# Cross-attention in 160 slots: the order of the low parts, the bias addition and the fill's last value pass

## The chip, the cores and the metric

One core of a Trainium2 chip. The metric is the device time of one execution in microseconds (us); of several runs the median counts. The engines are named as in the profile: PE (TensorE, matmuls) with PEld (its weight loads), DVE (VectorE), ACT (ScalarE), POOL (GpSimd) and SP (SyncE, which issues nearly all DMAs here).

## The reference

The inputs are x (32 batches of 512 rows of 640) and a context (32 batches of 77 rows of 1024). The context has exactly 77 rows, so the three further key segments of the reference are empty, and what is left is one attention with 20 heads of 32, an output projection, a bias and a residual:

```python
q = _heads(hidden_states @ to_q_w)
s = jnp.einsum('bhqd,bhkd->bhqk', q, k) * scale
p = jax.nn.softmax(s, axis=-1)
h = jnp.einsum('bhqk,bhkd->bhqd', p, v)
out = _merge(h) @ to_out_w + to_out_b
out = (out + residual) / RESCALE        # RESCALE = 1.0
```

Everything is float32. The kernel multiplies in the type fp32r and gets its precision back by splitting each operand into a high part (a cast to fp32r) and a low part (the operand minus its high part), and by adding three products: high with high, high with low, low with high.

## The kernel before, in words

**Ahead of the main loop** (up to about 265 us of the span) the keys and values of all batches are computed in four groups of columns, split, and written to scratch in DRAM (k_dram, v_dram). The main part then works in 160 slots, `slot(n)`, n = 5 b + j: b is the batch of 512 query rows and j one of five chunks of four heads.

**One slot** works on several stages at once, for different n:

- scores of slot n, four groups of 128 query rows, t = 0 to 3: three matmuls each (L464), then VectorE's negated row maximum (L472); `exps` runs four exponentials per group on ScalarE (L482), which also sum.
- queries of slot n+1: 15 matmuls (L445) in two portions of 6 and 9; `split_q` makes high (ScalarE, L102) and low (VectorE, L103).
- probabilities of slot n-1: `sums` takes the reciprocals on VectorE (L492), `normalize` multiplies on POOL (L497), `transpose_p` transposes 32x32 blocks on VectorE (L504) and writes them to DRAM with four DMAs (pd, L511).
- slot n-2's transposed probabilities are loaded again, `load_p`: three DMAs (L521, L523) into `raw`, three planes of 512.
- slot n-3 is "taken" (LAG = 3): `cast_p` makes the high parts of all three planes on ScalarE (L529); `rest_p` the low parts of planes 0 and 1 on VectorE (L535); `last_p` copies two quarters with POOL (L542, L543) and makes the low part of plane 2 there (lp, L545); `values` runs four matmuls into the bank pa (L554), reading planes 0, 1, 3 and 4 of pp in turn; `sum_a` adds four head quarters (ScalarE copy L578, two additions on VectorE, L580).
- slot n-4's last value pass: one more matmul with lp (`rest_values`, L566), after which `high_a` (ScalarE, L587) and `low_a` (VectorE, L592) leave the attention output `at`; `low_a` also frees pa, which has one buffer.
- output projection of an earlier batch: 24 matmuls per slot (L610) in two pieces after a fixed table (STEPS, CUTS, PIECES), into two PSUM banks `po`. `finish` adds a closed bank to the residual tile xr on VectorE (L639) and stores finished rows (L645). That residual is loaded one slot earlier (`load_residual`, L599), and POOL adds the bias to it (`add_bias`, L603), in the slots with j = 2, 3, 4 and 0.
- x of the next batch: loads (L251), transposes on VectorE (L255), `split_x` with high parts on ScalarE (L262) and low parts on POOL (L263), in the slots with j = 2 (two chunks) and j = 3 (three).
- keys and values of the next group are loaded into kb and vb by SP, `refill` in two halves (L417 in j = 1 and 2, L425 in j = 0 and 3); `copy_values` copies within vb on POOL in j = 1 and 4 (L433, L435).

[...] In the main loop the order ahead of scores group 1 is

```python
s = scores(n, 0)
if n:
    normalize(n - 1, sums(n - 1))
if taken is not None:
    rest_p(taken)
if taken is not None:
    last_p(taken)
```

with `cast_p` before it and `add_bias` far behind it, after the second half of `refill`, `finish` and `load_residual`.

**The fill** is the slots in which a value pass is taken but no projection is there yet: n = 3 to 6 (`filling`). Slot 7 (NC_ + 2) is the first with a projection. After the last slot `end()` works off what is left, with the same helpers.

## Time and profile before

| what | value |
| --- | --- |
| runs, median (lowest to highest) | 2008.37 us (2007.27 to 2008.49), 3 runs |
| the profiled execution, its own time | 2004.05 us |
| its span | 2002.3 us |
| instructions in it | 36798 |
| granted TensorE clock, mean | 0.993 |
| DMA | 448.34 MB, mean 224 GB/s |

The span runs from the first to the last instruction of the profiled execution; its own time is a little longer than the span, and lies just below the three timed runs. In the tables of the profile a row names line, engine, operation and tiles (out<-in) and gives times in us or ns; "idle before" is idle time of that engine just ahead of such instructions, with what ended it, and a releaser is inferred from the semaphores, so with several waits it is the one that came last.

### The profile page before, as it was taken

How to read it: one execution, taken by the hardware profiler on the slowest of the kernel's cores; microseconds unless marked ns; L12 is line 12 of the kernel's file. 1: busy time of each engine (PE TensorE's matmuls, PEld its weight loads, DVE VectorE, ACT ScalarE, POOL GpSimd, SP SyncE). 2: the span in 40 equal slices, each digit the busy share in tenths (PEclk: the TensorE clock that was granted, in tenths of full speed). 3: DMA queues.
4: the chain of work that ended last, by engine and by line, in shares of the span. 5: the costliest groups of instructions: out<-in, count | busy, mean ns of one | idle time of the engine just before them, and what ended most of it. 6: DMA issues, size and time to landing. Idle time of an engine off the chain costs nothing.

```text
span 2002.3 us, 36798 instructions
## 1 busy us (share of the span) xinstructions
PE 1896.2 (95%) x10172; PEld 1668.2 (83%) x10172; DVE 1596.7 (80%) x2334; ACT 1525.0 (76%) x6050; POOL 1448.0 (72%) x1308
## 2 busy tenths in 40 slices
PE   9999996999999999999999999999999999999997
PEld 7888985888888888888888888888888888888886
DVE  4444447888888888889888888888888888888885
ACT  3232247888888888888888888888888888888883
POOL 1000156788788888888888888888888888888875
PEclk9999997999999999999999999999999999999999
DMA  9888788888888888888888888888888888888975
GB/s 189 210 187 244 178 226 205 219 232 218 228 234 234 225 230 229 232 229 242 222 241 229 237 231 223 236 237 228 224 238 236 232 223 231 230 230 230 240 212 156
DMA packets 561436, 448.34 MB, mean 224 GB/s; under 512 B 177296, under 2 KB 459344, under 8 KB 561232
## 3 DMA queue, kind: packets, MB, share of 16 engines
q1 hardware_dynamic: 556720, 431.50, 83.0%
q0 software_dynamic: 4416, 14.34, 2.1%
q8 instruction: 82, 1.34, 0.3%
q14 instruction: 122, 1.00, 0.2%
q10 hardware_dynamic: 96, 0.16, 0.0%
HBM read 264.21 MB, written 181.64 MB: 223 GB/s over the span
## 4 chain that ended last, share of the span: by engine, by line
PE 30%; DMA 21%; ACT 20%; issue 12%; DVE 10%; SPq 5%; POOL 2%; DVEq 0%; ACTq 0%; POOLq 0%
PE pq L445 9%; ACT pn L482 8%; DMA raw<-pd 8%; DMA xs<-in_x_dram 8%; PE po L610 7%; ACT pp L529 6%; PE pv L190 4%; PE sc L464 4%; PE pk L190 4%; SPq L511 3%; ACT aw L578 3%; DMA pd<-z 3%; DVE z L504 3%; DVE nm L472 3%; ACT xt L262 2%
## 5 line engine op out<-in xcount | busy, mean ns | idle before, releaser
L482 ACT ACTIVATE pn<-sc,nm 128x77 f32<-128x77 f32 x2560 | 802.2, 335 | 205.2 <-DVE nm L472 201.2
L610 PE MATMUL po<-wo_s,at 128*128 128x320 f32 x3840 | 640.5, 312 | 54.3 <-DVE at L592 28.4
L610 PEld LDWEIGHTS po<-wo_s,at 128*128 128x128 f32 x3840 | 576.0, 188 | 79.8 <-DVE xr L639 41.8
L445 PE MATMUL pq<-xt,wq_s 128*128 128x512 f32 x2400 | 611.1, 396 | 0.0
L497 POOL TENSOR_TENSOR pn<-pn,rs 128x1232 f32<-128x1232 f32 x160 | 387.7, 2423 | 242.2 <-DVE rs L492 155.8
L482 ACT ACTIVATION_READ_ACCUMULATOR pn<-sc,nm 128x1 f32 x2560 | 545.9, 213 | 0.0
L445 PEld LDWEIGHTS pq<-xt,wq_s 128*128 128x128 f32 x2400 | 440.1, 190 | 76.9
L535 DVE TENSOR_TENSOR pp<-raw,pp 96x1024 fp32r<-96x1024 f32 x160 | 355.8, 2224 | 140.2 <-ACT pp L529 134.0
L464 PE MATMUL sc<-kb,qt 128*128 128x308 f32 x1920 | 380.6, 307 | 28.1 <-DMA kb<-k_dram 16.3
L464 PEld LDWEIGHTS sc<-kb,qt 128*128 128x128 f32 x1920 | 325.3, 189 | 77.2 <-ACT pn L482 13.9
L472 DVE TENSOR_REDUCE nm<-sc 128x4 f32<-128x308 f32 x640 | 294.0, 460 | 30.6 <-PE sc L464 27.5
L529 ACT CAST pp<-raw 128x1536 fp32r<-128x1536 f32 x160 | 237.5, 1484 | 30.2 <-DMA raw<-pd 27.7
L580 DVE TENSOR_TENSOR pa<-pa,aw 64x512 f32<-64x512 f32 x320 | 222.5, 695 | 47.2 <-ACT aw L578 38.9
L504 DVE STREAM_TRANSPOSE z<-pn 128x1280 f32<-128x1280 f32 x160 | 239.0, 1494 | 2.1 <-POOL pn L497 1.9
L263 POOL TENSOR_TENSOR xt<-xs,xt 128x512 fp32r<-128x512 f32 x160 | 202.7, 1292 | 35.8 <-ACT xt L262 35.5
L542 POOL CAST pp<-pp 32x512 fp32r<-32x512 f32 x160 | 211.0, 1319 | 18.9 <-ACT pp L529 8.4
L545 POOL TENSOR_TENSOR lp<-raw,pp 128x512 fp32r<-128x512 f32 x160 | 207.0, 1294 | 12.9
L603 POOL TENSOR_TENSOR xr<-xr,bias 128x640 f32<-128x640 f32 x128 | 200.7, 1569 | 2.5
L554 PE MATMUL pa<-pp,vb 128*128 128x512 f32 x640 | 176.9, 397 | 3.9 <-DVE at L592 2.1
L578 ACT COPY aw<-pa 64x1024 f32<-64x1024 f32 x160 | 161.8, 1011 | 20.3 <-PE pa L554 16.5
L211 POOL DMA_DIRECT2D k_dram<-ks x20 | 14.5, 727 | 190.0 <-DVE ks L103 190.0
L190 PE MATMUL pk<-ct,wk_s 128*128 128x512 f32 (+1 forms) x600 | 134.2, 382 | 1.7 <-ACT wk_s L102 0.9
(48 smaller groups left out, 1783.1 us busy)
## 6 DMA issues: line engine op xcount, KB each, us to landing
pd<-z SPq DMA_DIRECT2D x640, 160.0 KB, 3.5
raw<-pd SPq DMA_DIRECT2D x160, 512.0 KB, 4.2
xs<-in_x_dram SPq DMA_DIRECT2D x128, 320.0 KB, 6.0
raw<-pd SPq DMA_DIRECT2D x320, 128.0 KB, 4.2
xr<-in_x_dram SPq DMA_DIRECT2D x128, 320.0 KB, 4.2
out_dram<-xr SPq DMA_DIRECT2D x127, 320.0 KB, 3.8
v_dram<-vs SPq DMA_DIRECT2D x80, 192.0 KB, 4.1
k_dram<-ks POOLq DMA_DIRECT2D x20, 512.0 KB, 4.1
```

The source lines that it names most:

```text
L190: nc.tensor.matmul(held[j][:, :gn], w[:, k, a, :], cts[g, k][:, c, :gn], start=(k == 0 and n == 0), stop=(k == NK - 1 and n == 2),)
L445: nc.tensor.matmul(pqs[n], wq_s[:, k, a, j * P : (j + 1) * P], xts[b, k][:, c, :], start=(k == 0 and m == 0), stop=(k == NC_ - 1 and m == 2),)
L464: nc.tensor.matmul(sc[:, :KCOLS], qt[:, a, t * P : (t + 1) * P], kb[:, j - GROUPS[g][0], c], start=(m == 0), stop=(m == 2),)
L472: nc.vector.tensor_reduce(nm, sc[:, :KCOLS].rearrange("p (h k) -> p h k", k=NKEY), AX.X, ALU.max, negate=True)
L482: nc.scalar.activation(pnb[n % 2][:, at, :NKEY], sc[:, i * NKEY : (i + 1) * NKEY], AF.Exp, bias=nm[:, i : i + 1], accum_out=sms[n][:, at : ...
L497: nc.gpsimd.tensor_tensor(pf, pf, rs.unsqueeze(2).to_broadcast([P, NQ * HPC, NKEY]), ALU.mult)
L504: nc.vector.transpose(z.rearrange("p b t j -> p t b j"), pn.rearrange("p (t h) k -> p t (h k)", t=NQ).rearrange("p t (b i) -> p t b i", i=Q),)
L529: nc.scalar.copy(pp[:, 0:3, :], raws[n])
L535: nc.vector.tensor_tensor(pp[:96, 3:5, :], raw[:96, 0:2, :], pp[:96, 0:2, :].bitcast(F32), ALU.subtract)
L578: nc.scalar.copy(aw, pa[64:])
L580: nc.vector.tensor_tensor(pa[64 * p : 64 * p + 64, 0], pa[:64, p], aw[:, p], ALU.add)
L610: nc.tensor.matmul(pos[b, t, h][:, :HALF], ats[b * NC_ + j][:, a, t * P : (t + 1) * P], wos[0][:, j, c, h * HALF : (h + 1) * HALF], start= ...
```

## The change

It changes the order in the slot, and one cast:

- `cast_p`: the cast of three planes becomes two instructions, planes 0 and 1 first, then plane 2.
- `slot`: `rest_p` (L535, VectorE) moves ahead of the reciprocals of `sums` (L492) and so ahead of `normalize` in program order; the two are on VectorE and POOL.
- `add_bias` moves from after `load_residual` to right after scores group 0, ahead of `rest_p`, `normalize` and `last_p`; on POOL it is now ahead of L497. The tile it adds to is the same, loaded in the slot before.
- fill: the last value pass and `high_a`, `low_a` (`taken_parts`) come after the second portion of the queries instead of around scores group 1, in slots with `filling` and in slot 7 (`FIRST_OUT`); in the fill slot with j = 1 both halves of `refill` (four DMAs of keys) come right after the first portion of the queries, ahead of `load_p`.

```diff
     def cast_p(n):
 
         pp = late[0].tile([P, 5, S], FPR, tag="pp", name="pp", bufs=1)
-        nc.scalar.copy(pp[:, 0:3, :], raws[n])
+        nc.scalar.copy(pp[:, 0:2, :], raws[n][:, 0:2, :])
+        nc.scalar.copy(pp[:, 2, :], raws[n][:, 2, :])
         pps[n] = pp
...
     LATE = 2
+    FIRST_OUT = NC_ + 2
     LAG = 3
...
         s = scores(n, 0)
+        if j in BIAS and b >= BIAS[j][0]:
+            add_bias(b - BIAS[j][0], BIAS[j][1])
+        if taken is not None:
+            rest_p(taken)
         if n:
             normalize(n - 1, sums(n - 1))
-        if taken is not None:
-            rest_p(taken)
         if taken is not None:
             last_p(taken)
...
         if ahead:
             queries(n + 1, 0, 2)
-        if n - 1 in takes:
+        if filling and j == 1:
+            refill(b, j, 0)
+            refill(b, j, 1)
+        late_rest = filling or n == FIRST_OUT
+        if n - 1 in takes and not late_rest:
             rest_values(takes[n - 1])
         s = scores(n, 1)
-        if n - 1 in takes:
+        if n - 1 in takes and not late_rest:
             taken_parts(takes[n - 1], rest=False)
         if n - LAG + 1 in pds and n > LATE:
             load_p(n - LAG + 1)
-        if filling:
+        if filling and j != 1:
             refill(b, j, 0)
...
-        refill(b, j, 1)
+        if not (filling and j == 1):
+            refill(b, j, 1)
         finish()
...
-        if j in BIAS and b >= BIAS[j][0]:
-            add_bias(b - BIAS[j][0], BIAS[j][1])
         exps(n, 1, *s)
...
             queries(n + 1, 2, NC_)
+        if n - 1 in takes and late_rest:
+            taken_parts(takes[n - 1])
         s = scores(n, 2)
```

## The prediction

> **What bounds the kernel now.** I read the page's busy shares first, then the busy time by stretch for the steady part, then TensorE's timeline over one batch, and last the other engines' timelines over the same batch. First the row of the busy shares, then the row of the steady stretch (us, then busy time and instructions of PE, PEld, DVE, ACT and POOL, granted clock, DMA share, GB/s).

> ```profile
> PE 1896.2 (95%) x10172; PEld 1668.2 (83%) x10172; DVE 1596.7 (80%) x2334; ACT 1525.0 (76%) x6050; POOL 1448.0 (72%) x1308
> ```

> ```profile
> 376.00:1909.00 1533.00, 1462.69 (x8120) 1298.94 (x8119) 1337.01 (x1943) 1313.25 (x5366) 1273.59 (x1131) 1.00 0.87 231
> ```

> A steady batch issues 5 x 56 = 280 matmuls, so 8120 of them are 29 batches: 1533/29 = 52.86 us each. TensorE is the busiest engine, at full clock, but no slot kind is full by itself; where it still waits is seen in one batch. I call a slot by its j, kind 0 to 4, and give times from its first scores matmul (L464). Columns: start, duration, engine, line; in brackets the idle time.

> ```profile
> 1381.54 0.59 PE L464 MATMUL sc<-kb,qt 128*128 128x308 f32 x3
> ...
> 1388.28 1.09 PE L554 MATMUL pa<-pp,vb 128*128 128x512 f32 x4
> 1389.21 0.59 PE L464 MATMUL sc<-kb,qt 128*128 128x308 f32 x3
> ...
> 1391.30 1.14 PE L610 MATMUL po<-wo_s,at 128*128 128x320 f32 x6 [0.64 <-DVE xr L639]
> 1392.28 0.59 PE L464 MATMUL sc<-kb,qt 128*128 128x308 f32 x3
> ...
> 1397.27 2.29 PE L610 MATMUL po<-wo_s,at 128*128 128x320 f32 x12
> ...
> 1402.51 0.59 PE L464 MATMUL sc<-kb,qt 128*128 128x308 f32 x3
> ...
> 1405.04 0.47 PE L566 MATMUL pa<-lp,vb 128*128 128x512 f32 x1 [0.55 <-ACT pp L529]
> ...
> 1410.06 1.10 PE L554 MATMUL pa<-pp,vb 128*128 128x512 f32 x4
> ...
> 1413.17 0.58 PE L464 MATMUL sc<-kb,qt 128*128 128x308 f32 x3
> ...
> 1419.74 0.86 PE L610 MATMUL po<-wo_s,at 128*128 128x320 f32 x4 [1.13 <-DVE at L592]
> 1420.44 1.09 PE L554 MATMUL pa<-pp,vb 128*128 128x512 f32 x4
> ...
> 1424.43 0.59 PE L464 MATMUL sc<-kb,qt 128*128 128x308 f32 x3
> ...
> 1434.28 0.59 PE L464 MATMUL sc<-kb,qt 128*128 128x308 f32 x3
> ```

> The differences of the L464 rows are the slots: 10.74, 10.23, 10.66, 11.26 and 9.85 us. Every slot has the same 56 matmuls, and kind 4 runs without a gap, so 9.85 is TensorE's own time and 52.86 - 5 x 9.85 = **3.6 us of waiting per batch**. Here it is 0.89 in kind 0 (a projection bank that L639 empties), 0.38 in kind 1 (the same, inside the 2.29), 0.81 in kind 2 (L566 adds into the bank that the sums L580 write; the row names a cast beside it), 1.41 in kind 3 (the low part L592). All four end with an instruction of VectorE (in other batches kind 1 also waits for keys, in kind 2's stead). Why VectorE is late there:

> ```profile
> 1383.43 0.23 DVE L492 RECIPROCAL rs<-sm 128x16 f32<-128x16 f32 x1
> 1384.40 2.70 DVE L535 TENSOR_TENSOR pp<-raw,pp 96x1024 fp32r<-96x1024 f32 x1 [0.74 <-ACT pp L529]
> ...
> 1390.78 0.47 DVE L639 TENSOR_TENSOR xr<-po,xr 128x320 f32<-128x320 f32 x1
> ...
> 1405.34 1.15 DVE L535 TENSOR_TENSOR pp<-raw,pp 96x1024 fp32r<-96x1024 f32 x1
> ...
> 1415.54 3.16 DVE L535 TENSOR_TENSOR pp<-raw,pp 96x1024 fp32r<-96x1024 f32 x1 [1.10 <-ACT pp L529]
> ```

> ```profile
> 1381.75 1.57 POOL L603 TENSOR_TENSOR xr<-xr,bias 128x640 f32<-128x640 f32 x1
> 1383.74 2.28 POOL L497 TENSOR_TENSOR pn<-pn,rs 128x1232 f32<-128x1232 f32 x1 [0.42 <-DVE rs L492]
> 1386.09 1.49 POOL L542 CAST pp<-pp 32x512 fp32r<-32x512 f32 x1
> 1387.63 0.61 POOL L543 CAST pp<-pp 32x512 fp32r<-32x512 f32 x1
> ...
> 1405.56 3.07 POOL L497 TENSOR_TENSOR pn<-pn,rs 128x1232 f32<-128x1232 f32 x1 [3.94 <-PE pa L566]
> ...
> 1412.85 2.54 POOL L263 TENSOR_TENSOR xt<-xs,xt 128x512 fp32r<-128x512 f32 x2
> ...
> 1422.76 3.79 POOL L263 TENSOR_TENSOR xt<-xs,xt 128x512 fp32r<-128x512 f32 x3
> ```

> The low parts L535 take 1.15 us when they start before the normalization L497 (1405.34, 0.22 ahead of it), and L497 then takes 3.07 instead of 2.28. When L497 is already running, L535 ends 1.08 after it whatever it started with: 1384.40 + 2.70 = 1387.10 against 1383.74 + 2.28 = 1386.02. So the two exclude each other, and the copy L542 pays too (1.49 against 0.61 for L543 of the same shape). In kind 0 L535 ends at 5.56 and VectorE then runs back to back to L639 (end 1391.25); in kind 3 it ends at 5.53 and L592 follows. **The present order makes VectorE pay for the normalization.**

> [...]

> **The change, part by part.** *Low parts ahead of the reciprocals, the cast in two parts.* The chain to the next values is now serial: values of the slot before, sums copy L578, four exponentials, first part of the cast, L535, L492, L497, L542, L543, values. Its remaining durations:

> ```profile
> 1411.25 1.01 ACT L578 COPY aw<-pa 64x1024 f32<-64x1024 f32 x1
> 1412.16 0.62 ACT L262 CAST xt<-xs 128x512 fp32r<-128x512 f32 x1
> ...
> 1414.02 1.49 ACT L529 CAST pp<-raw 128x1536 fp32r<-128x1536 f32 x1
> ```

> ```profile
> L482 ACT ACTIVATE pn<-sc,nm 128x77 f32<-128x77 f32 x2560 | 802.2, 335 | 205.2 <-DVE nm L472 201.2
> ...
> L472 DVE TENSOR_REDUCE nm<-sc 128x4 f32<-128x308 f32 x640 | 294.0, 460 | 30.6 <-PE sc L464 27.5
> ```

> The cast parts cost about 1.01 + 0.62 (by their widths, 1024 and 512) against 1.49: 0.14 more on ScalarE, 0.48 less before L535 can start. ScalarE hides the 0.14 in the 201.2 us it now waits for the reductions; uncovered it would be 160 x 0.14 = 22 us. Values start at 1410.06 in kind 2 and L578 at 1411.25, 1.2 later. So part one ends 1.2 + 1.01 + 4 x 0.335 + 1.01 = 4.5 after the values' start V; with V = 6.74 (1388.28 - 1381.54) that is 11.25, or 1.4 into the next slot of 9.85. Then L535 1.15, L492 0.23, L497 2.28, two copies 0.61 each and 0.2 of gaps: L543 ends 5.1 later, at **6.5**. L492 now waits behind L535, which waits for the cast; behind it in VectorE's queue stand the second reduction and L592, which come at about 3 to 4 instead of 5.5.

> Only the fourth values matmul reads what L543 writes (line 553); four take 1.09 with their overlap, so it starts some 0.7 after the first. That they wait singly is seen in the fill, where values start before L543 has ended (335.86); the third fence is the fill's key loads, for below:

> ```profile
> 335.76 1.20 PE L554 MATMUL pa<-pp,vb 128*128 128x512 f32 x4 [1.02 <-DVE at L592]
> 343.60 1.11 PE L464 MATMUL sc<-kb,qt 128*128 128x308 f32 x3 [6.64 <-DMA kb<-k_dram]
> ```

> ```profile
> 335.25 0.61 POOL L543 CAST pp<-pp 32x512 fp32r<-32x512 f32 x1
> ```

> ```profile
> 338.01 2.03 SPq L417 DMA_DIRECT2D kb<-k_dram  x4
> ```

> So L543 may end up to 7.4 in kinds 0, 1, 2 and 4. In kind 3 fewer projections stand ahead: V is 1420.44 - 1413.17 less the wait of 1.41, 5.86, and the limit 6.55; there ScalarE also has an L262 (0.62) on the chain, L543 comes at 7.1, and 0.55 is waited. The waits for L580, L592 and L639 go, but for one: in kind 0 L639 still follows the last scores and their reduction, 1389.21 + 0.59 + 0.46 + 0.47 = 1390.73 at the earliest against 1391.25 now, so 0.5 of the 0.89 goes and some 0.35 stays (limits 0 and 0.89).

> *Bias first in the slot.* It puts 1.57 us ahead of L497, after the wait for the residual's landing; everything of POOL's queue stands behind it: L497, the copies, lp (L545), L263. SP's rows in kind 4, and the landing of that one L599:

> ```profile
> 1427.48 0.38 SPq L521 DMA_DIRECT2D raw<-pd  x1
> ...
> 1430.23 0.49 SPq L599 DMA_DIRECT2D xr<-in_x_dram  x1
> ```

> ```profile
> DMA to landing us min/median/max: 7.2/7.2/7.2
> ```

> Kind 0's residual is issued at 1430.23, behind two loads of x, and lands at 1437.43, 3.15 into the slot. Its queue waits at L521 for the transposed probabilities; VectorE being about 1.5 earlier in kind 3, I take landing at 1.2 to 1.7. The POOL operation against L535 is not in the trace: from below it costs nothing, from above it excludes like L497. I take the latter, by the rows of L497 and L542, which both exclude.
> - Kind 0: bias and L535 run one behind the other from 1.2 to 3.9, L497 from 4.0, L543 at 7.65 to 7.8: 0.4 too late at most, plus the 0.35 of L639: **0.7** (0.3 to 1.25).
> - Kind 1 has no bias addition: **0**.
> - Kind 2: no x loads stand ahead of its residual, it comes about when the scores do, L543 at 7.1 to 7.5: **0.15** (0 to 0.6).
> - Kind 3: the two L263 of kind 2 end at 2.2 now (1412.85 + 2.54), and at about 1.2 without a bias addition ahead of them but with the copies later; bias until 2.8, L535 until 3.9, L497 from 4.2, L543 at 7.85: **1.3** (0.55 to 1.5).
> - Kind 4: the three L263 of kind 3 end at 2.1 now (1422.76 + 3.79) and by the same rule at 1.0 to 1.6; then L535 and bias exclude each other until 4.1, L543 at 7.8: **0.45** (0 to 0.9).

> Sum 2.6 against 3.6: **1.0 less per batch**, over 29 + 1 batches 29 us; since the five waits are not independent (a late slot passes its lateness on through the values' start) I take 25.

> *Fill.* The key loads of the first kind 1 slot move ahead of L521, into a time in which SP only waits; they issue some 4 us before the row's 338.01, and of the wait of 6.64 above some 4 go. Moving the last value pass behind the queries takes L566 off TensorE's way, but those slots wait for L592 and the copies instead (the 1.02 above), and there the serial chain costs 0.7 to 1.3 in two slots. Together **-2** (-6 to +3). The end of the program casts in two parts three times: 0. No DMA is added.

> **The sum**: -25 - 2 = -27. The profiled execution took 2004.05 (span 2002.3 and 1.75 around it), so 1977; the runs' median is 4.3 above it, so **1981 us**.

> **Rivals.** *(a) Slower: the bias addition waits for its residual.* If the residuals land as late as now, kind 0's bias runs from 3.15 to 4.7, L497 until 7.0, L543 ends at 8.35: 0.95 + 0.3; kind 2 gives 0.6, kind 3 1.5, kind 4 0.9, together 4.2 against 3.6: 30 x 0.6 = +18, less 2: 2024. It decides against the change when the five waits pass 3.6. For it: the x loads ahead of L599. Against it: VectorE frees SP's queue earlier. *(b) Much faster:* the bias addition costs nothing, as it falls into POOL's idle time (the L497 of 1405.56 has 3.94 of it before it) or does not exclude L535: waits 0.3, 0, 0, 0.8 and 0.4 for the L263, 1.5 in all: 30 x 2.1 = 63 less, 1943. *(c) No change:* DMA takes the gain. Its share is already 0.87, and 1.0 us less per batch makes it 0.89; if loads of keys then come late, the time stays at 2006.

> **Numbers.** Forecast 0.5 (alone 1966 to 1998), (a) 0.26, (b) 0.10, (c) 0.14. The range leaves out most of (b) and the end of (a): 1958 to 2022. A measurement of this kernel tells about 0.2% from no change, 4 us: faster 0.61, within 0.13, slower 0.26.

> **What would show it.** Right: L535 at 1.15 in most slots with L497 after it, L592 before 5 in kind 3, no wait of TensorE for L639 in kind 1 or for L592, and new waits at L554 in kinds 3 and 4 for L543. Wrong: L603 waiting for DMA ahead of L497 beyond 2 us in kind 0 or 2; L535 near 2.5 beside L603; or waits at L464 for keys.

## The result and the profile after

The changed kernel took **1987.23 us** (median of 4 runs, 1986.02 to 1988.17), the kernel before 2008.43 us on the same chip (4 runs, 2007.27 to 2010.18): a ratio of 0.989, with a 95% interval of 0.988 to 0.991. The forecast was 1981. The profiled execution took 1987.78 us, 16.3 less than that of before.

In the changed kernel's listing everything from the second line of `cast_p` on stands one line lower: low parts L536, copies L543 and L544, values L555, last value pass L567, low part of the output L593, bias addition L604, projections L611, finishing addition L640.

First the row of the busy shares, then that of the steady stretch, which holds 29 batches as before (start:end, length, then busy time of PE, PEld, DVE, ACT and POOL, clock, DMA share, GB/s).

```profile
PE 1913.4 (96%) x10172; PEld 1662.6 (84%) x10172; DVE 1522.6 (77%) x2334; ACT 1547.2 (78%) x6210; POOL 1365.4 (69%) x1308
```

```profile
372.40:1895.80 1523.40, 1479.51 (x8122) 1292.47 (x8121) 1273.03 (x1944) 1334.29 (x5512) 1200.69 (x1132) 1.00 0.87 232
```

A batch takes 1523.4/29 = 52.53 us instead of 52.86: only 0.34 us less. The gain of 16.4 us in the span splits into 3.5 ahead of slot 10 (it starts at 372.6 instead of 376.1), 9.9 in the steady stretch (1533.3 to 1523.4, unrounded starts) and 3.0 behind it. VectorE lost 74 us of busy time and GpSimd 83; TensorE still waits 52.53 - 49.25 = **3.28 us per batch**, against 3.6. The waits have changed their place, as the groups of instructions show (busy, mean ns of one | idle ahead of them and what ended most of it).

```profile
L611 PE MATMUL po<-wo_s,at 128*128 128x320 f32 x3840 | 624.7, 310 | 4.0 <-DVE xr L640 0.8
...
L497 POOL TENSOR_TENSOR pn<-pn,rs 128x1232 f32<-128x1232 f32 x160 | 364.4, 2277 | 241.3 <-DVE rs L492 101.8
...
L604 POOL TENSOR_TENSOR xr<-xr,bias 128x640 f32<-128x640 f32 x128 | 252.8, 1976 | 73.8 <-DMA xr<-in_x_dram 67.3
L536 DVE TENSOR_TENSOR pp<-raw,pp 96x1024 fp32r<-96x1024 f32 x160 | 253.5, 1584 | 41.4 <-ACT pp L529 38.4
...
L555 PE MATMUL pa<-pp,vb 128*128 128x512 f32 x640 | 222.0, 430 | 47.1 <-POOL pp L543 23.4
...
L555 PEld LDWEIGHTS pa<-pp,vb 128*128 128x128 f32 x640 | 114.7, 189 | 122.4 <-POOL pp L544 56.2
```

The projections waited 54.3 us for VectorE before (L610) and wait 4.0 now: that bound is gone. In its place the values wait for GpSimd's two copies. The low parts, 2224 ns on average before, take 1584, and the normalization, 2423 before, is at 2277. But the bias addition, 1569 ns before with 2.5 us of idle time ahead of it, takes 1976 and waits 67.3 us for the residual. One batch on TensorE, kinds 0 to 4 from the first to the last row:

```profile
1369.52 0.59 PE L464 MATMUL sc<-kb,qt 128*128 128x308 f32 x3
...
1376.25 1.47 PE L555 MATMUL pa<-pp,vb 128*128 128x512 f32 x4
...
1380.09 0.59 PE L464 MATMUL sc<-kb,qt 128*128 128x308 f32 x3
...
1389.94 0.59 PE L464 MATMUL sc<-kb,qt 128*128 128x308 f32 x3
...
1398.04 0.49 PE L555 MATMUL pa<-pp,vb 128*128 128x512 f32 x1 [0.18 <-POOL pp L544]
...
1400.56 0.59 PE L464 MATMUL sc<-kb,qt 128*128 128x308 f32 x3
...
1407.78 0.50 PE L555 MATMUL pa<-pp,vb 128*128 128x512 f32 x1 [0.73 <-POOL pp L543]
1408.45 0.50 PE L555 MATMUL pa<-pp,vb 128*128 128x512 f32 x1 [0.17 <-POOL pp L544]
...
1411.85 0.59 PE L464 MATMUL sc<-kb,qt 128*128 128x308 f32 x3
...
1419.68 0.50 PE L555 MATMUL pa<-pp,vb 128*128 128x512 f32 x1 [0.17 <-POOL pp L544]
...
1422.20 0.58 PE L464 MATMUL sc<-kb,qt 128*128 128x308 f32 x3
```

The slots are 10.57, 9.85, 10.62, 11.29 and 10.35 us long. Kind 1 is now free of gaps, kind 4 no longer is, and kind 3 is as long as before (11.26) with a wait for GpSimd in the place of the one for VectorE. GpSimd and VectorE in the same kinds 2 to 4 say why:

```profile
1391.39 3.01 POOL L604 TENSOR_TENSOR xr<-xr,bias 128x640 f32<-128x640 f32 x1 [1.62 <-DMA xr<-in_x_dram]
1394.37 2.28 POOL L497 TENSOR_TENSOR pn<-pn,rs 128x1232 f32<-128x1232 f32 x1
...
1401.83 1.57 POOL L604 TENSOR_TENSOR xr<-xr,bias 128x640 f32<-128x640 f32 x1
1404.78 2.28 POOL L497 TENSOR_TENSOR pn<-pn,rs 128x1232 f32<-128x1232 f32 x1 [1.38 <-ACT at L588]
1407.12 0.61 POOL L543 CAST pp<-pp 32x512 fp32r<-32x512 f32 x1
...
1409.73 3.79 POOL L263 TENSOR_TENSOR xt<-xs,xt 128x512 fp32r<-128x512 f32 x3
1413.49 2.55 POOL L604 TENSOR_TENSOR xr<-xr,bias 128x640 f32<-128x640 f32 x1
1416.01 2.27 POOL L497 TENSOR_TENSOR pn<-pn,rs 128x1232 f32<-128x1232 f32 x1
```

```profile
1391.76 1.21 DVE L536 TENSOR_TENSOR pp<-raw,pp 96x1024 fp32r<-96x1024 f32 x1
...
1402.49 1.98 DVE L536 TENSOR_TENSOR pp<-raw,pp 96x1024 fp32r<-96x1024 f32 x1 [0.82 <-ACT pp L529]
...
1412.97 1.64 DVE L536 TENSOR_TENSOR pp<-raw,pp 96x1024 fp32r<-96x1024 f32 x1
```

In these rows the bias addition and the low parts exclude each other, in both directions. In kind 3 L604 runs first (1401.83 to 1403.40), and L536 ends 1.07 after it, at 1404.47, though it began at 1402.49. In kind 2 the low parts go first (end 1392.97) and the addition ends 1.43 after them, at 1394.40. In kind 4 L536 waits for L263, which ends at 1413.52, and the addition ends 1.43 after L536 again. Whichever way it falls, both stand ahead of L497, and behind that follow the copies that the values wait for.

### The profile page after: what moved, and what is told of

The parts are those of the page before. It is cut to its first block, busy times and chain, and to the rows that moved or that the text cites. A ratio compares the mean times of both kernels' runs of the same rounds, so it can differ in the third digit from the quotient of the medians.

```text
span 1985.9 us, 37062 instructions
## 1 busy us (share of the span) xinstructions
PE 1913.4 (96%) x10172; PEld 1662.6 (84%) x10172; DVE 1522.6 (77%) x2334; ACT 1547.2 (78%) x6210; POOL 1365.4 (69%) x1308
## 3 DMA queue, kind: packets, MB, share of 16 engines
q14 instruction: 124, 1.02, 0.2%
## 4 chain that ended last, share of the span: by engine, by line
PE 48%; DMA 12%; POOL 12%; issue 10%; ACT 8%; DVE 6%; SPq 3%; POOLq 0%; DVEq 0%; ACTq 0%
PE po L611 14%; PE pq L445 13%; PE sc L464 7%; POOL pn L497 6%; PE pv L190 4%; PE pa L555 4%; DMA xr<-in_x_dram 4%; PE pk L190 4%; ACT pn L482 3%; DMA pd<-z 3%; POOL pp L544 2%; DMA raw<-pd 2%; ACT aw L579 2%; POOL xr L604 2%; ACT pp L529 2%
## 5 line engine op out<-in xcount | busy, mean ns | idle before, releaser
L482 ACT ACTIVATE pn<-sc,nm 128x77 f32<-128x77 f32 x2560 | 804.1, 335 | 82.2 <-DVE nm L472 76.6
L611 PE MATMUL po<-wo_s,at 128*128 128x320 f32 x3840 | 624.7, 310 | 4.0 <-DVE xr L640 0.8
L611 PEld LDWEIGHTS po<-wo_s,at 128*128 128x128 f32 x3840 | 576.1, 188 | 13.6 <-DVE xr L640 12.0
L482 ACT ACTIVATION_READ_ACCUMULATOR pn<-sc,nm 128x1 f32 x2560 | 545.0, 213 | 0.0
L497 POOL TENSOR_TENSOR pn<-pn,rs 128x1232 f32<-128x1232 f32 x160 | 364.4, 2277 | 241.3 <-DVE rs L492 101.8
L472 DVE TENSOR_REDUCE nm<-sc 128x4 f32<-128x308 f32 x640 | 292.0, 457 | 133.8 <-PE sc L464 130.1
L464 PE MATMUL sc<-kb,qt 128*128 128x308 f32 x1920 | 378.7, 306 | 9.6 <-ACT pn L482 3.5
L464 PEld LDWEIGHTS sc<-kb,qt 128*128 128x128 f32 x1920 | 325.9, 189 | 49.6 <-ACT pn L482 9.1
L604 POOL TENSOR_TENSOR xr<-xr,bias 128x640 f32<-128x640 f32 x128 | 252.8, 1976 | 73.8 <-DMA xr<-in_x_dram 67.3
L536 DVE TENSOR_TENSOR pp<-raw,pp 96x1024 fp32r<-96x1024 f32 x160 | 253.5, 1584 | 41.4 <-ACT pp L529 38.4
L504 DVE STREAM_TRANSPOSE z<-pn 128x1280 f32<-128x1280 f32 x160 | 241.3, 1508 | 55.1 <-POOL pn L497 50.4
L555 PE MATMUL pa<-pp,vb 128*128 128x512 f32 x640 | 222.0, 430 | 47.1 <-POOL pp L543 23.4
L263 POOL TENSOR_TENSOR xt<-xs,xt 128x512 fp32r<-128x512 f32 x160 | 202.9, 1294 | 32.2 <-ACT xt L262 32.2
L555 PEld LDWEIGHTS pa<-pp,vb 128*128 128x128 f32 x640 | 114.7, 189 | 122.4 <-POOL pp L544 56.2
L529 ACT CAST pp<-raw 128x1024 fp32r<-128x1024 f32 x160 | 168.9, 1056 | 5.2 <-DMA raw<-pd 4.2
```

Source lines behind the costliest of these rows:

```text
L464: nc.tensor.matmul(sc[:, :KCOLS], qt[:, a, t * P : (t + 1) * P], kb[:, j - GROUPS[g][0], c], start=(m == 0), stop=(m == 2),)
L472: nc.vector.tensor_reduce(nm, sc[:, :KCOLS].rearrange("p (h k) -> p h k", k=NKEY), AX.X, ALU.max, negate=True)
L482: nc.scalar.activation(pnb[n % 2][:, at, :NKEY], sc[:, i * NKEY : (i + 1) * NKEY], AF.Exp, bias=nm[:, i : i + 1], accum_out=sms[n][:, at : ...
L497: nc.gpsimd.tensor_tensor(pf, pf, rs.unsqueeze(2).to_broadcast([P, NQ * HPC, NKEY]), ALU.mult)
L504: nc.vector.transpose(z.rearrange("p b t j -> p t b j"), pn.rearrange("p (t h) k -> p t (h k)", t=NQ).rearrange("p t (b i) -> p t b i", i=Q),)
L536: nc.vector.tensor_tensor(pp[:96, 3:5, :], raw[:96, 0:2, :], pp[:96, 0:2, :].bitcast(F32), ALU.subtract)
```

## The experiments

Theory: moving the low parts ahead is all of the gain; the bias addition in front takes part of it back, because it stands on GpSimd ahead of the chain normalization, copies, values. Rivals: the bias addition in front costs nothing, and the serial chain alone takes the rest; or the transfers do. Ratios are to the kernel before in runs on the same chip (medians there 2002.40 to 2003.72 us, 2008.43 on the chip of the first measurement, so absolute times in the expectations are to be compared by ratio). The changed kernel itself was measured with that first pair and the experiments apart from it; where ratios and traces give different sizes for a step between them, both are named. The table holds the mean length of a slot of each kind in the 29 steady batches of each profile, from the starts of the slots' first L464, and their sum; TensorE's own time is 9.85. A wait that is named below with a kind and a time is a mean over these batches: by how much the step between two matmuls is longer than the same step in kind 4 of the kernel before.

| kernel | ratio | 95% | kind 0 | 1 | 2 | 3 | 4 | batch |
| --- | --- | --- | --- | --- | --- | --- | --- | --- |
| before | 1 | | 10.74 | 10.93 | 10.27 | 11.07 | 9.85 | 52.87 |
| changed | 0.9893 | 0.9876–0.9911 | 10.59 | 10.03 | 10.26 | 11.30 | 10.35 | 52.53 |
| e1: bias back | 0.9826 | 0.9811–0.9841 | 10.44 | 10.37 | 9.91 | 10.79 | 10.35 | 51.86 |
| e2: no bias | 0.9787 | 0.9771–0.9803 | 10.44 | 11.01 | 9.92 | 10.54 | 9.85 | 51.76 |
| e3: low parts alone | 0.9889 | 0.9869–0.9909 | 10.41 | 10.41 | 9.89 | 11.01 | 10.35 | 52.07 |
| e4: fill alone | 0.9995 | 0.9985–1.0005 | 10.74 | 10.79 | 10.32 | 11.13 | 9.85 | 52.83 |
| e5: whole cast | 0.9953 | 0.9937–0.9969 | 10.87 | 10.05 | 10.09 | 11.25 | 10.35 | 52.62 |
| e6: bias first alone | 0.9958 | 0.9942–0.9974 | 11.00 | 10.22 | 10.40 | 10.69 | 10.35 | 52.67 |
| e7: residual ahead | 0.9895 | 0.9879–0.9910 | 10.43 | 10.08 | 10.22 | 11.29 | 10.35 | 52.38 |
| e8: copies ahead | 1.0191 | 1.0174–1.0208 | 14.11 | 10.63 | 9.87 | 9.96 | 9.85 | 54.43 |
| e9: but not in kind 0 | 1.0003 | 0.9985–1.0021 | 12.87 | 10.14 | 9.94 | 10.31 | 9.85 | 53.10 |
| e10: e9, bias back | 0.9868 | 0.9839–0.9898 | 11.07 | 11.20 | 10.10 | 9.87 | 9.85 | 52.09 |
| e11: e10 and two edits | 0.9804 | 0.9782–0.9825 | 10.70 | 10.40 | 11.02 | 9.87 | 9.85 | 51.84 |
| e12: copies ahead in 3 | 0.9769 | 0.9749–0.9788 | 10.06 | 10.57 | 9.96 | 9.87 | 10.96 | 51.43 |

### The change taken apart (e1 to e6)

**e1**, the changed kernel with the bias addition back behind the residual's load:

```diff
         s = scores(n, 0)
-        if j in BIAS and b >= BIAS[j][0]:
-            add_bias(b - BIAS[j][0], BIAS[j][1])
...
             load_residual(b - RESIDUAL[j][0], RESIDUAL[j][1])
+        if j in BIAS and b >= BIAS[j][0]:
+            add_bias(b - BIAS[j][0], BIAS[j][1])
```

> The changed kernel with the bias addition back in its old place. Theory: the bias addition ahead of the normalization is what gave most of the gain back; without it the waits of TensorE fall from the 3.3 us per batch of the changed kernel to about 1.6 to 2.0 (kind 0 0.35, kind 3 0.8, kind 4 0.4, a little for keys), so some 1.4 x 30 = 42 us less: about 1945 us. Rival: the chain of values, cast, low parts, reciprocals, normalization and copies is serial and sets those waits whatever POOL does first; then the time stays within 8 us of 1987.

The move costs 0.67% of the time by the ratios, some 13 us; by the traces it costs 20 (52.53 - 51.86 = 0.67 us in each of 29 batches, and 20.5 us between the spans of 1985.9 and 1965.4). That is the theory's direction and a third to a half of its 42 us. The groups of e1's profile:

```profile
L497 POOL TENSOR_TENSOR pn<-pn,rs 128x1232 f32<-128x1232 f32 x160 | 364.2, 2276 | 317.1 <-DVE rs L492 175.9
...
L263 POOL TENSOR_TENSOR xt<-xs,xt 128x512 fp32r<-128x512 f32 x160 | 232.5, 1479 | 31.4 <-ACT xt L262 31.4
...
L604 POOL TENSOR_TENSOR xr<-xr,bias 128x640 f32<-128x640 f32 x128 | 200.9, 1571 | 2.5
```

At its old place the bias addition waits for nothing, and GpSimd's idle time ahead of L497 grows from 241.3 to 317.1 us. The gain comes out of kinds 3 (0.51 less) and 2 (0.35 less); kind 1 gives 0.34 back, where TensorE now waits for keys.

**e2**, the changed kernel without the bias addition; the bias is left out of the output:

```diff
     def add_bias(b, t):
-        nc.gpsimd.tensor_tensor(xrs[b, t], xrs[b, t], bias, ALU.add)
+        pass
```

> The changed kernel without any bias addition (the bias is left out of the sum, so this part of the computation is missing; loads and stores stay). Theory: the whole price of the bias addition on POOL; a little under the kernel with the addition in its old place, about 1925 to 1940 us, with L535's counterpart at 1.2 us nearly everywhere. Rival (the serial chain sets the waits): 1975 to 1987 us.

Neither number came: 0.9787 is 1.1% below the changed kernel and only 0.4% below e1, so in its old place the addition costs little, 0.4% net. With it gone, kind 1 waits 0.66 for keys and kind 0 0.56 for its projection bank. What the prediction's rival (b) takes as free gain is met by the next two limits.

**e3**, the kernel before with only the low parts moved:

```diff
         s = scores(n, 0)
+        if taken is not None:
+            rest_p(taken)
         if n:
             normalize(n - 1, sums(n - 1))
-        if taken is not None:
-            rest_p(taken)
```

> The kernel before with one edit: the low parts ahead of the reciprocals; cast whole, bias addition and fill as before. Theory: this edit carries the gain: the waits behind VectorE (3.6 us per batch) go, and about 1.8 for the copies are left: 2008 - 54 = 1955 us. Rival: the order of these two alone gains little (under 12 us) since the low parts then wait 0.48 longer for the whole cast and the normalization comes later still: 1996 to 2008 us.

This one edit gives 0.9889, what the whole change gives (0.9893), and a shorter steady batch (52.07 against 52.53). Its groups:

```profile
L610 PE MATMUL po<-wo_s,at 128*128 128x320 f32 x3840 | 625.0, 310 | 5.2 <-DVE xr L639 1.4
...
L535 DVE TENSOR_TENSOR pp<-raw,pp 96x1024 fp32r<-96x1024 f32 x160 | 220.8, 1380 | 113.1 <-ACT pp L529 105.8
```

The low parts fall from 2224 to 1380 ns, and the projections' waits from 54.3 to 5.2 us. The 1.1% are 22 us, between the theory's 54 and the rival's under 12: the waits for the copies are left, 1.14 us in kind 3 alone. The rest of the change nets nothing by the ratios and costs 9 us by the spans (1976.9 against 1985.9): what the fill and the split cast add, the bias takes.

**e4**, the kernel before with only the fill's two edits (the last value pass and its two parts behind the queries, and the keys' loads ahead of `load_p`, as in the change's diff).

> The kernel before with the fill's edits alone (value pass behind the queries in slots 3 to 7, four key loads ahead in the first slot of kind 1). Theory from the two traces, in which slot 7 starts 5.3 us earlier: -5 us, 2003 us. Rival, as predicted: -2 us, 2006 us, because the 5.3 come in part from the other edits.

Nothing measurable. TensorE in its fill:

```profile
339.82 2.08 PE L554 MATMUL pa<-pp,vb 128*128 128x512 f32 x4 [3.03 <-DVE at L592]
...
351.04 0.57 PE L610 MATMUL po<-wo_s,at 128*128 128x320 f32 x2 [2.22 <-ACT at L587]
```

The wait of 6.64 us for keys (L464 at 343.60 in the kernel before) is gone, slot 7 starts at 341.7 instead of 343.6, and the later L592 and L587 give it back: slot 10 starts at 376.2 against 376.1. Beside the other parts the same edits are worth more: slot 10 starts at 370.2 in e1 and at 375.9 in e3, which lacks them and the split cast.

**e5**, the changed kernel with the cast in one instruction:

```diff
-        nc.scalar.copy(pp[:, 0:2, :], raws[n][:, 0:2, :])
-        nc.scalar.copy(pp[:, 2, :], raws[n][:, 2, :])
+        nc.scalar.copy(pp[:, 0:3, :], raws[n])
```

> The changed kernel with the cast of the low parts' operand in one instruction again. Theory (the part cast lets the low parts start about 1 us earlier, but TensorE waits for the copies behind the normalization anyway, so little of it arrives): between the bias-back kernel (0.9826) and the kernel with only the low parts moved (0.9889) stood 0.2 us per batch of the split; the whole cast costs about 6 us over the changed kernel, ratio 0.992. Rival (the split cast is what lets the low parts in ahead of the bias addition): over 15 us, ratio 0.997 or more. Other rival: no difference, 0.989.

By the ratio the split is worth 0.6%, between theory and rival. The trace shows less: a batch of 52.62 instead of 52.53, 29 x 0.09 = 2.6 us, and 3.0 us between the two profiled executions. I take the sign as shown and the size as open.

**e6**, the kernel before with only the bias addition moved to the front (the change's lines of `add_bias`).

> The kernel before with the bias addition first in the slot as its only edit; the low parts stay behind the reciprocals. Theory (the bias addition costs GpSimd 1.6 to 2 us wherever it stands, and in front it pushes normalization, copies and so the values' inputs back, in kinds 3 and 0 first): slower than before by 5 to 25 us, ratio 1.003 to 1.012. Rival (the bias addition at the slot's end was in the way of the low parts of the next slot, and in front it is not): faster than before by 10 to 30 us, ratio 0.985 to 0.995.

The rival is right: alone, the move gains 0.4%. Its groups:

```profile
L497 POOL TENSOR_TENSOR pn<-pn,rs 128x1232 f32<-128x1232 f32 x160 | 465.0, 2906 | 127.9 <-DVE rs L492 113.6
...
L535 DVE TENSOR_TENSOR pp<-raw,pp 96x1024 fp32r<-96x1024 f32 x160 | 291.4, 1821 | 88.5 <-ACT pp L529 88.2
```

The low parts fall from 2224 to 1821 ns and the normalization rises from 2423 to 2906. The addition in front delays the normalization's start, and the low parts get in ahead of it. So this move does a part of what moving the low parts does, and the two don't add up: once the low parts stand ahead, only its cost is left, which is e1's 13 to 20 us. The rival's words named another way (the addition out of the way at the slot's end); the rows speak for this one.

### What holds the rest back (e7 to e12)

**e7**, the residual's load ahead of the two loads of x on SP's queue in kind 4:

```diff
-        if j == 4 and b and b + 2 < B:
-            load_x(b + 2, (0, 1))
         if j in RESIDUAL and b >= RESIDUAL[j][0]:
             load_residual(b - RESIDUAL[j][0], RESIDUAL[j][1])
+        if j == 4 and b and b + 2 < B:
+            load_x(b + 2, (0, 1))
```

> The changed kernel with the residual's load ahead of the two loads of x on SyncE's queue in kind 4, so that kind 0's residual lands earlier than the median of 1.55 us after its slot's start. Theory (kind 0's wait of 0.40 us per batch for the copies stands behind a bias addition that waits for its landing): that wait goes, 0.4 x 30 = 12 us less than the changed kernel, ratio 0.983. Rival (the chain on GpSimd is serial, and the addition has no slack even with its residual there): same as the changed kernel, 0.989.

Kind 0 gets 0.16 shorter, a batch 0.15, some 4 us, which the ratio does not show (0.9895). The late residual is a small part; the chain behind it is the larger one.

**e8**, the copies ahead of the normalization on GpSimd; **e9**, the same in kinds 1 to 4 only (`copy_p` holds L543 and L544, taken out of `last_p`):

```diff
         if taken is not None:
             rest_p(taken)
+            copy_p(taken)
         if n:
             normalize(n - 1, sums(n - 1))
```

> The changed kernel with GpSimd's two copies that the values wait for ahead of the normalization, which is left where it was. Theory (the values wait only because the copies stand behind the normalization, 2.3 us, on GpSimd's queue): the waits of the values, 2.7 us per batch, go, and with them up to 2.7 x 30 = 80 us if nothing else is late; keys (0.4 us in kind 1) and the split of x (0.3 in kind 4) come back as in the bias-back kernel, so 40 to 60 us less than the changed kernel, ratio 0.960 to 0.970. Rival (the copies wait for the low parts' or the cast's end and hold the normalization up behind them, and the transposes and the products are late in their place): within 10 us of the changed kernel, 0.984 to 0.994.

> The changed kernel with the two copies ahead of the normalization in kinds 1 to 4; kind 0 keeps the changed kernel's order. Theory (copies ahead takes the values' waits away, and its loss of 4.3 us per batch sits in kind 0 alone, where the normalization's lateness makes the transposes and the finishing additions late): kind 0 is again as in the changed kernel, 10.6 us, kinds 1 to 4 take 39.9 to 40.3 us, so a batch of about 50.7 instead of 52.5 us, 55 us less, ratio 0.958 to 0.966. Rival (GpSimd as a whole is what the loss shows: copies that run beside the low parts take twice as long in every kind, and the delay arrives in kind 0 from kind 4 before it): kind 0 stays over 12.5 us and the ratio over 0.985.

The values' waits do go: kinds 2 to 4 of e8 run at 9.85 to 9.96. But kind 0 loses 3.5 us, e8 as a whole is 1.9% slower than the kernel before, outside both ranges, and e9, with kind 0's order put back, still has 12.87 there: that order is not the cause. GpSimd, VectorE and TensorE in e8, from kind 4 into kind 0:

```profile
1402.01 1.49 POOL L543 CAST pp<-pp 32x512 fp32r<-32x512 f32 x1
1403.56 0.61 POOL L544 CAST pp<-pp 32x512 fp32r<-32x512 f32 x1
1404.25 2.28 POOL L497 TENSOR_TENSOR pn<-pn,rs 128x1232 f32<-128x1232 f32 x1
```

```profile
1406.56 1.51 DVE L504 STREAM_TRANSPOSE z<-pn 128x1280 f32<-128x1280 f32 x1 [1.67 <-POOL pn L497]
1408.00 0.65 DVE L103 TENSOR_TENSOR qt<-pq,qt 128x512 fp32r<-128x512 f32 x1
...
1408.96 0.47 DVE L644 TENSOR_TENSOR xr<-po,xr 128x320 f32<-128x320 f32 x1
1409.47 1.43 DVE L585 TENSOR_TENSOR pa<-pa,aw 64x512 f32<-64x512 f32 x2
```

```profile
1408.70 0.41 PE L464 MATMUL sc<-kb,qt 128*128 128x308 f32 x1 [0.25 <-DVE qt L103]
...
1411.04 0.47 PE L571 MATMUL pa<-lp,vb 128*128 128x512 f32 x1 [0.53 <-DVE pa L585]
...
1420.24 1.49 PE L615 MATMUL po<-wo_s,at 128*128 128x320 f32 x6 [1.79 <-DVE xr L644]
```

(In the kernels from e8 on, L571 is the last value pass, L585 the sums, L615 the projections and L644 the finishing addition.) The copies start behind the low parts and take 2.2 us; the normalization ends that much later, the transposes wait for it in VectorE's queue, and all that stands behind them there is late: the queries' low part, the finishing addition, the sums. e9's rival is right in its two bounds and in that the delay arrives in kind 0 from kind 4: there e9 waits 0.7 us at L571 and 0.56 at the scores, besides 1.13 at the values, which have no copies ahead in that kind. Some of e8's loss is the clock's: its mean is 0.978 against 0.994 in the changed kernel, from which I estimate 0.016 x 2038 = 33 us (last section). The ten steady batches of e8 that ran at full clock throughout take 53.11 us, and e9's take 53.10, so in the steady part e9 gains over e8 no more than the clock had cost.

**e10**, e9 with the bias back as in e1; **e11**, e10 with two edits more (kind 1's second half of keys right behind the first, at the slot's start; the first piece and its finishing additions ahead of the transposes in kind 0 as in kind 3):

```diff
+            if j == 1:
+                refill(b, j, 1)
...
-        if j == 3 and has_out:
+        if j in (0, 3) and has_out:
             piece(bo_, first)
             finish()
```

> The same, with the bias addition back at its place behind the residual's load. Theory (the bias addition ahead of the low parts costs its time on GpSimd ahead of the copies and the normalization): 5 to 15 us less again, ratio 0.953 to 0.961. Rival (with the copies ahead, nothing waits for GpSimd's start of the slot any more): same as the run before, within 0.002.

> The same, with the first pieces of the output and their finishing additions ahead of the transposes in kind 0 too, as kind 3 has them, and with both halves of the keys' load at the start of kind 1. Theory (kind 0's wait for a bank, 0.35 to 0.38 us, hangs on the finishing additions behind the transposes, and kind 1's wait for keys, up to 0.4 us, on their issue behind other loads): both go, 0.7 x 30 = 20 us less than the run before, ratio about 0.948. Rival (the keys are late by the transfer, not by their issue, and the finishing additions hold the transposes up): no more than 5 us less.

e10 takes 1.35% off e9, 27 us where 5 to 15 were expected, and with 0.9868 stays behind e1 and far from 0.953 to 0.961: kind 1 waits 1.25 us for keys and kind 0 0.7 at L571. e11 takes 0.64% off, 13 of the 20 us that were expected (0.9804, not 0.948). Its bank wait (kind 0) and its key wait (kind 1) are gone, but kind 2 then waits 1.08 us at L571 for the sums: what the keys had hidden.

**e12**, e1 with the copies ahead in kind 3 alone and e11's two edits:

> The bias addition back behind the residual's load, the copies ahead of the normalization in kind 3 alone, and the two edits of the run before (finishing additions ahead of the transposes in kind 0, both halves of the keys at the start of kind 1). Theory (ahead of the normalization the copies pay only where the values are waited for by more than the slot after them can lose: that is kind 3, 0.93 us; in kinds 4, 1 and 0 the third value pass of the next slot then waits for its operand, 0.7 to 1.1 us): kinds 0 and 1 about 10.05, kind 2 9.9, kind 3 9.9, kind 4 10.3, a batch of 50.2 to 50.8 us instead of 51.86 with the bias back alone, 30 to 50 us less, ratio 0.958 to 0.968. Rival (what is taken from one wait is late at the next, as in the three runs before): within 10 us of the bias-back kernel, 0.977 to 0.987.

0.9769, 0.6% below e1, so the rival's bound and not the theory's 0.958 to 0.968; it is the fastest of all these kernels, 2.3% below before. Kinds 0, 2 and 3 came out as expected. Kind 1 waits 0.4 us for the copies and 0.3 at a projection where it had waited for keys, and in kind 4 stands the largest wait:

```profile
1375.19 1.49 POOL L543 CAST pp<-pp 32x512 fp32r<-32x512 f32 x1
...
1382.44 4.77 POOL L263 TENSOR_TENSOR xt<-xs,xt 128x512 fp32r<-128x512 f32 x3
```

```profile
1387.27 0.73 PE L445 MATMUL pq<-xt,wq_s 128*128 128x512 f32 x2 [0.61 <-POOL xt L263]
```

The queries of the next slot wait for the low parts of x, which run on GpSimd behind the copies, the normalization and the bias addition, and take 4.77 instead of 3.79 us (an L536 of 1384.69 to 1386.07 lies beside them).

## Why the prediction was right, and by how much not

- *Low parts ahead.* Right, and by e3 all of the net gain. L611's waits fell from 54.3 to 4.0 us, and kind 0 keeps 0.34 for L640 as worked out. But L536 runs at 1.21 only where it goes first, in 60 of the 145 steady slots and not in most, as the prediction's sign had it. And not all of the 3.6 us hung on VectorE: over all steady batches the kernel before waited 0.66 us each for keys in kind 1, which the prediction names only in a parenthesis; 0.18 of that is left.
- *The values wait for the copies in kinds 3 and 4.* Right: 1.3 and 0.45 were said, 1.45 and 0.50 came; in kind 0 0.7 and 0.74.
- *Kinds 1 and 2* are the terms mis-sized most: 0 and 0.15 were said, 0.18 and 0.41 came. In kind 1 it is keys; in kind 2 the bias addition waits for its residual and is then stretched to 3.01 by the low parts, which puts L497 at 1394.37, 4.4 into the slot. All five together are 3.28 instead of 2.6, so 0.34 less per batch instead of 1.0, 10 us instead of 25. (With its rounded 1.0 the prediction's 30 batches give 30 us and not 29; it went on with 25, so nothing hangs on it.)
- *The fill.* Up to slot 10 there are 3.5 us of gain (2 were said) and behind the steady stretch 3.0 (0 was said); by e4 the fill's edits alone give none of it, so the 3.5 come of them and the other parts together. The median fell by 21 us where the profiled executions differ by 16. These two made the forecast of 1981 come closer than its steady term, and that was luck.
- *The bias excludes the low parts.* Taken as an upper bound for want of a row; the rows above show it. Rival (b), that it costs nothing, falls by e1: in front it costs 13 to 20 us.
- *The bias waits for its residual,* rival (a): it does, for 67.3 us in all; in the steady batches 16.6 stand in kind 0 and 43.5 in kind 2. e7 gives only some 4 us for kind 0's. Kind 2's, where the prediction saw no x loads ahead, lands 1.1 us into the slot (median): in the batch shown it is issued at 1387.21, behind L521, L523 and the keys' second half on SP's queue. No run moved that one, so what it costs stays open. *DMA takes the gain,* rival (c): not in the changed kernel, where the share stays at 0.87; in e1, e2 and e10 the wait for keys in kind 1, 0.36, 0.66 and 1.25 us against 0.18, takes a part back.
- What stays open: the size of the split cast's worth (2.6 us by the steady trace, 12 by the ratios), and what a version would reach in which the low parts of x are not behind the bias addition; it was not tried.

## What to carry to other kernels

When two operations exclude each other in the trace, as the low parts did with the normalization and with the bias addition here, order them by who is waited for: the operation whose result the bound engine reads goes first, and anything with slack goes into the idle time behind it, not in front (e1, 0.9826, against the changed kernel's 0.9893). Before an operation is moved ahead in an engine's order, follow what it pushes back through the next engine's order too: the copies ahead of the normalization freed the values (9.87 to 9.96 us in kinds 2 and 3 of e8, 10.26 and 11.30 in the changed kernel) and made the transposes, and all behind them, late (kind 0 at 14.11 instead of 10.59, a part of it the clock's). And two edits that shorten the same operation need not add up: the low parts ahead gave 1.1% alone (e3), the bias addition in front 0.4% alone (e6), and the whole change, which holds both, 1.1%. Measure each alone.

## What the runs showed of the hardware

**In e8 the clock halved after some waits of TensorE and not after others as long.** After the wait of 1.79 us at 1420.24, the same matmuls run slower (1.49 for six L615 where 1.04 was usual). In the traces of the kernel before and of the changed kernel the granted clock is 1.00 or 0.50 and nothing else, and the times at which it changes lie whole multiples of 3.41 us apart (in the kernel before it is 0.50 from 304.24 to 314.48, from 338.37 to 348.62 and from 505.63 to 509.04). Two pairs of neighbouring windows of that grid in e8, with TensorE's busy time first and the granted clock in the third column from the right:

```profile
1417.42:1420.83 3.41, 1.62 (x12) 1.36 (x11) 3.41 (x5) 1.98 (x8) 1.11 (x1) 1.00 0.98 238
1420.83:1424.25 3.42, 3.42 (x12) 3.04 (x11) 3.20 (x5) 2.97 (x13) 1.46 (x2) 0.50 0.79 177
...
1308.19:1311.60 3.41, 1.72 (x12) 1.46 (x12) 3.41 (x5) 1.98 (x8) 1.13 (x1) 1.00 0.75 245
1311.60:1315.02 3.42, 3.42 (x20) 3.01 (x20) 3.13 (x6) 2.68 (x11) 0.63 (x1) 1.00 0.79 175
```

**The start of a record does not always say who goes first.** L604's record of 1391.39 begins 0.37 ahead of that of L536 (1391.76), and yet it is L536 that runs at 1.21 and L604 that stretches to 3.01; with 0.66 ahead (1401.83 against 1402.49) L604 goes first. The changed kernel has 63 pairs in which L604's record begins first and the two overlap. From 0.42 us ahead on, L604 goes first in all of them; of the ten that begin 0.08 to 0.40 ahead, it goes first in five and L536 in five. In the kernel before, L497 goes first in all 20 pairs that begin 0.17 to 0.20 ahead of L535. So in the changed kernel the operation whose record begins first goes first in 58 of these 63 pairs; what decides the other five is not shown.
